# First ticks of layer 0: another order of transposes, folds, gates, logits, flags and loads

## The chip, the cores and the metric

The kernel is one program on one core of a Trainium2 chip. The metric is the device time in microseconds (us) of one execution; lower is better. Five engines run side by side, each with its own list of instructions that it works off in order: TensorE (PE, with its weight loads shown as PEld), VectorE (DVE), ScalarE (ACT), GpSimd (POOL) and SyncE (SP), which here only issues DMAs. Matrix products go from SBUF through PE into PSUM, and ACT or DVE read them from there.

## The reference

The input x (8 sequences of 256 tokens, 128 wide) goes through four layers, and all of them attend to one context ctx of 8 x 64 rows, 64 wide. All data are float32. Layer 0 is what the change touches:

```python
logits = x @ ent_w.T + ent_b                       # one number per token
aw = softmax(logits over the 256 tokens)
read_mask = -sum(aw * log(aw + 1e-9)) > 1.0        # one flag per sequence
q = x @ Wq.T;  k = ctx @ Wk.T + pos;  v = ctx @ Wv.T   # 16 heads of 8
attn = softmax(q k^T * 8**-0.5)                    # over the 64 context rows
memory_output = (attn v) @ Wo.T
pooled = mean of ctx over its 64 rows
h1 = silu([x, pooled] @ gate_w1.T + gate_b1)
gate = sigmoid(h1 @ gate_w2.T + gate_b2)           # one number per token
x = where(read_mask, layernorm(x + gate * memory_output), x)
```

Layer 1 is attention with one head over the same context and adds its result to x. Layer 2 is six times masked self-attention with 16 heads of 64, cross-attention to the context, and a feed-forward block. Layer 3 is one small attention and a last layer norm.

## The kernel before

**Tiles.** x lives in SBUF as `t`, 16 tiles of 128 tokens. For layer 0 it is also turned, into `xT` (128 x 2048), four tiles (one chunk, two sequences) at a time. Products of weights are folded once, before they are used per sequence. `fold_l0` (L513) makes `WVO` from Wv and Wo: it spreads Wo over the 16 heads on POOL (L517), transposes Wv (L522), copies the result twice on ACT (L525), multiplies (L532) and copies from PSUM (L539). `fold_l1`, `fold_l1_values` and `values_l1` (L544 to L589) do the like for layer 1.

**Ticks and phases.** The work is not written in the order in which it runs. `at(tick, phase, fn)` puts a small function into a plan, and at the end of the program the plan is sorted by tick, then phase. Every instruction that a function emits on PE, DVE, ACT or POOL is made to follow the previous one of the plan on that engine (L1199 to L1211). So on these four engines the plan is the order, and an instruction that waits holds up everything behind it on its engine. SP is not in this order; DMAs stand there as the scheduler of the framework puts them.

Sequence b of layer 0 starts at tick 2b: its queries (L635) and its keys spread over heads (POOL, L643) two ticks earlier, then per tick one block of 128 queries: scores (PE, L328, phase 1), lower (ACT copies the scores, L357, DVE takes the maximum, L359, POOL subtracts it, L360, phase 2), exps (ACT, L366, phase 8), a tick later divide (DVE sum L370 and reciprocal L371, POOL product L372), then turn (DVE, L380), then sums (PE, L388). `make_values` (L303, L309) needs `WVO`; `add` (L655) needs `gate`, `normal` and `mix` (L666, L685) need `nflag` and `flag`. Layer 1 of sequence b follows from tick 2b + 7, and the first self-attention projects its keys in tick 13.

The start of the program is `plan_start` (L614). In tick -4 `turn_x` (L431) turns all of x and makes the keys of layer 0 (`k0T`, L407 and L411). In tick 0, after the first scores, come `logits` (L440: DVE builds a selector, PE L447, then DVE and ACT make the softmax, L453 to L459) and `gate_inputs` (L474: mean of the context, L476 and L477, a small product L479, then the hidden values of the gate on PE, L486). In tick 1 come `entropy` (L462, with a logarithm on ACT, L465), `gate_hidden` (L492: for each of eight sequences a sigmoid on ACT, L497, and a multiply on DVE, L498), `fold_l0`, and `gates` (L500: flags, L503, gates, L505, and a sigmoid, L509), then the conversion of the self-attention mask (DVE, L602) and its store to DRAM (SP, L609).

**Buffers.** All PSUM tiles are two banks wide and come from one pool of four, so each new tile waits until the readers of the fourth before it are done. The tags `k`, `q`, `v`, `e` and `o` of SBUF also have four tiles each; the four incoming pieces of the mask take two of `k` and two of `q`. Small operands of the start are cut from two tiles with `place` (L92).

**Loads.** SP issues x, then the constants one after the other, the mask (L190), and the weights of layer 2; ACT's queue issues the context, and the key, position and query weights of layer 0.

Of the kernel before, what the change touches and what calls it, by code (L numbers as in the profile page):

```python
# [16 lines left out]
P = 128  # L17
# [10 lines left out]
def tile_xattn_stack(ctx: ExitStack, tc: tile.TileContext, io, out: bass.AP):  # L28
# [16 lines left out]
    def two_banks(base):  # L45
        return psum.tile([P, 1024], F32, tag="ps", name=uniq(base))
# [4 lines left out]
    def tp_tile():  # L51
        return one_bank("tp")

    def mm_tile():
        return one_bank("mm")

    def big(tag, bufs=4, shape=(P, 1024), dtype=F32):

        return heap.tile(list(shape), dtype, tag=tag, name=uniq(tag), bufs=bufs)
# [4 lines left out]
    def sm(shape, tag):  # L64
        return small.tile(shape, F32, tag=tag, name=uniq(tag))

    def load_const(name, shape):
        t_ = const.tile(shape, F32, tag=name, name=name)
        nc.sync.dma_start(out=t_, in_=io[name])
        return t_  # L70
# [7 lines left out]
    def column(name):  # L78
        v = io[name]
        t_ = const.tile([v.shape[0], 1], F32, tag=name, name=name)  # L80
        nc.sync.dma_start(out=t_, in_=v.unsqueeze(1))
        return t_
# [9 lines left out]
    def place(where, n, rows=P):  # L92
        whole, used = room[where]
        room[where][1] = used + n
        assert used + n <= whole.shape[-1]
        return whole[:rows, used : used + n]

    def load_into(where, name, rows, n, queue=None):
        t_ = place(where, n, rows)
        (queue or nc.sync).dma_start(out=t_, in_=io[name])  # L100
        return t_
# [20 lines left out]
    w0k = load_into("second", "L0_WkT", DM, D, nc.scalar)  # L122
    posT = load_into("second", "L0_posT", D, M, nc.scalar)
    w0q = load_into("second", "L0_WqT", D, D, nc.scalar)
    entw = load_const("L0_entT", [D, 1])
    entb = bcast_rows("L0_ent_b", B)
    w1b = load_into("second", "L0_w1bT", DM, 64)
# [2 lines left out]
    w2g = load_const("L0_w2T", [64, 1])  # L130
    b2g = bcast_rows("L0_gate_b2")
    w0v = load_into("second", "L0_WvT", DM, D)
    w0o = load_into("second", "L0_WoT", D, D)
    nc.sync.dma_start(out=ctx2[DM:], in_=ctx_v)
    ln0_g = column("L0_ln_scale")
    ln0_b = column("L0_ln_bias")

# [43 lines left out]
    for r in range(2):  # L181
        rows = slice(64 * r, 64 * r + 64)
        nc.vector.tensor_copy(hmask8[rows], hmask[rows, 8 * r : 8 * r + 8])


    mask_v = io["mask_BxSxS_ik0"].rearrange("b (h p) k -> p b h k", p=P)
    mask_in = []
    for i, tag in enumerate("kkqq"):
        mask_in.append(big(tag, shape=(P, 2, QT, S), dtype=I32))
        nc.sync.dma_start(out=mask_in[i], in_=mask_v[:, 2 * i : 2 * i + 2])  # L190


    W = {}
# [88 lines left out]
    def copy_to(out_, in_, on_vector=False):  # L282
        if on_vector:
            nc.vector.tensor_copy(out_, in_)
        else:
            nc.scalar.copy(out_, in_)  # L286
# [133 lines left out]
    def small_keys(where, w, bias=None):  # L420
        out_ = place(where, B * M).rearrange("p (b m) -> p b m", b=B)
        keys(w, out_, bias)
        return out_
# [4 lines left out]
    nflag = const.tile([P, B], F32, tag="nflag", name="nflag")  # L428
    cg = const.tile([64, B], F32, tag="cg", name="cg")

    def turn_x():  # L431
        for c in range(NT // 4):
            ps = tp_tile()
            for j in range(4):
                nc.tensor.transpose(ps[:, j * P : (j + 1) * P], t[:, 4 * c + j, :], ident)
            copy_to(xT[:, c * 512 : (c + 1) * 512], ps, c % 2 == 0)
            if c == 1:
                S0["k0T"] = small_keys("second", w0k)

    def logits():  # L440
        esel = place("second", B * B).rearrange("p (a b) -> p a b", a=B)
# [20 lines left out]
    def entropy():  # L462
# [8 lines left out]
        S0["rdiag"] = sm([B, B], "rdiag")  # L471
        nc.vector.tensor_scalar(S0["rdiag"], ident[:B, :B], read, None, ALU.mult)

    def gate_inputs():  # L474
        pooled = sm([DM, B], "pooled")
        nc.vector.tensor_reduce(pooled, ctx_all, AX.X, ALU.add)  # L476
        nc.vector.tensor_scalar(pooled, pooled, 1.0 / M, None, ALU.mult)  # L477
        cg_ps = mm_tile()
        nc.tensor.matmul(cg_ps[:64, :B], lhsT=w1b, rhs=pooled, start=True, stop=True)  # L479
        nc.vector.tensor_scalar(cg, cg_ps[:64, :B], b1g, None, ALU.add)  # L480
        S0["h"] = []
        for half in range(2):
            ps = two_banks("mm")
            for i in range(2):
                c = 2 * half + i
                nc.tensor.matmul(  # L486
                    ps[:64, i * 512 : (i + 1) * 512], lhsT=w1a,
                    rhs=xT[:, c * 512 : (c + 1) * 512], start=True, stop=True,
                )
            S0["h"].append(ps)  # L490
# [8 lines left out]

    def gates():  # L500

        ps = two_banks("mm")
        nc.tensor.matmul(ps[:, 512 : 512 + B], lhsT=ones, rhs=S0["rdiag"], start=True, stop=True)  # L503
        for n in range(NT):
            nc.tensor.matmul(  # L505
                ps[:, n : n + 1], lhsT=S0["hs"][n // 8][:64, (n % 8) * P : (n % 8 + 1) * P],
                rhs=w2g, start=True, stop=True,
            )
        nc.scalar.activation(gate, ps[:, :NT], AF.Sigmoid, bias=b2g)  # L509
        nc.vector.tensor_copy(flag, ps[:, 512 : 512 + B])  # L510
        nc.vector.tensor_scalar(nflag, flag, -1.0, 1.0, ALU.mult, ALU.add)

    def fold_l0():  # L513


        wobd = place("first", H * D).rearrange("p (h d) -> p h d", h=H)
        nc.gpsimd.tensor_tensor(  # L517
            wobd, w0o.unsqueeze(1).to_broadcast([P, H, D]),
            hmask.unsqueeze(2).to_broadcast([P, H, D]), ALU.mult,
        )  # L520
        tps = tp_tile()
        nc.tensor.transpose(tps[:, :DM], w0v, ident[:DM, :DM])  # L522
        wv2 = place("second", P)
        for r in range(2):
            nc.scalar.copy(wv2[:, r * DM : (r + 1) * DM], tps[:, :DM])  # L525
        S0["WVO"] = sb([P, HC, D], "WVO", 1, heap)
        wvo = S0["WVO"].rearrange("p (g a) d -> p a g d", g=2)
        for half in range(2):
            ps = two_banks("mm")
            for i in range(2):  # L530
                a = 2 * half + i
                nc.tensor.matmul(  # L532
                    ps[:, i * 512 : (i + 1) * 512], lhsT=wv2,
                    rhs=wobd[:, 4 * a : 4 * a + 4].rearrange("p h d -> p (h d)"),
                    start=True, stop=True,
                )
            for r in range(2):
                rows = slice(r * DM, (r + 1) * DM)
                nc.scalar.copy(  # L539
                    wvo[rows, 2 * half : 2 * half + 2],  # L540
                    ps[rows].rearrange("p (a g r d) -> p a g r d", a=2, g=2, r=2)[:, :, :, r, :],
                )

    def fold_l1():  # L544

        scale = float(D) ** -0.5
        k1T = S0["k1T"] = small_keys("third", w1k, b1k)
        tps = tp_tile()
        nc.tensor.transpose(tps[:, :P], w1q, ident)
        wqT = place("second", P)  # L550
        nc.scalar.mul(wqT, tps[:, :P], scale)
        ps = mm_tile()
        nc.tensor.matmul(
            ps, lhsT=wqT, rhs=k1T.rearrange("p b m -> p (b m)"), start=True, stop=True
        )
        S0["K1q"] = place("third", B * M).rearrange("p (b m) -> p b m", b=B)
        nc.scalar.copy(S0["K1q"].rearrange("p b m -> p (b m)"), ps)
        S0["bqb"] = place("fourth", P)
        nc.vector.tensor_scalar(S0["bqb"], b1q.to_broadcast([P, P]), scale, None, ALU.mult)

    def fold_l1_values():
        tps = tp_tile()
        nc.tensor.transpose(tps[:, :DM], w1v, ident[:DM, :DM])
        wvT = place("second", DM)
        nc.scalar.copy(wvT, tps[:, :DM])
        bvb = place("second", P)
        nc.vector.tensor_copy(bvb, b1v.to_broadcast([P, P]))
        ps = two_banks("mm")
        nc.tensor.matmul(ps[:DM, :D], lhsT=wvT, rhs=w1o, start=True, stop=True)
        nc.tensor.matmul(ps[:, 512 : 512 + D], lhsT=bvb, rhs=w1o, start=True, stop=True)  # L570
        wvo = place("second", D)
        bvo = place("second", D)
        nc.scalar.copy(wvo[:DM], ps[:DM, :D])
        nc.scalar.copy(bvo, ps[:, 512 : 512 + D])
        S0["wvo1"], S0["bvo"] = wvo, bvo
# [36 lines left out]
            )  # L612

    def plan_start():  # L614
        at(-4, 0, turn_x)
        at(0, 3.0, logits)
        at(0, 3.2, gate_inputs)
        at(1, 3.0, entropy)
        at(1, 3.1, gate_hidden)
        at(1, 3.2, fold_l0)  # L620
        at(1, 3.4, gates)
        for i in range(4):
            at(1, 8.5, lambda i=i: mask(i))
        at(1, 8.6, store_masks)
        at(3, 4, fold_l1)
        at(4, 4, fold_l1_values)
        at(5, 4, values_l1)
        at(16, 6, mask_keys)

    def plan_l0(b, T):  # L630
# [638 lines left out]
```

## Time and profile before

| what | value |
|---|---|
| median of 3 runs | 2530.57 us (2528.28 to 2533.17) |
| the profiled execution | 2528.09 us, of which the span 2526.4 us |
| busy: PE, PEld, DVE, ACT, POOL | 2393.0, 1765.0, 1822.0, 1735.1, 1443.0 us |
| mean granted PE clock | 0.975 |
| chain that ended last, by engine | PE 69%, POOL 13%, DVE 8%, ACT 7%, issue 3% |
| from 0 to 89.9 us | PE busy 60.51, granted clock 0.83 |
| from 89.9 to 300 us | PE busy 199.39, granted clock 0.98 |
| from 300 us to the end (2226.4 us) | PE busy 2133.09, granted clock 0.98 |

The page of the profile divides the span into 40 slices of 63 us and gives each engine's busy share in tenths. The chain that ended last is followed back from the last instruction, at each step to what released it. A row of a wait names the waiting group and its line, the group that released it, the time in all, how often, and the longest. A row of the timeline gives start and duration in us, engine, line, operation, what is written and read, how often, and in brackets the idle time ahead of it and what ended that. PE counts each float32 matmul of the program as two instructions.

### The profile page before, as it was taken

The page shows a single profiled execution, that of the slowest core. Times are in us where ns is not written, and L with a number is a line of the kernel's source. Part 1 is how long each engine was busy: PE and PEld are TensorE (multiplying, and loading weights), DVE is VectorE, ACT ScalarE, POOL GpSimd, SP SyncE. Part 2 cuts the span into 40 slices and gives each one's busy share as a digit, 9 for nine tenths or more (in the row PEclk, how much of TensorE's full clock was granted, in tenths as well). Part 3 has the DMA queues.
Part 4 walks back from the last instruction along what each step waited for, and adds up shares of the span by engine and source line. Part 5 has one row for each costly group of instructions (what it writes and reads, how often), then busy time and mean ns, then how long its engine had stood idle before and what let it go on. Part 6 is the DMA issues. An engine that isn't in the chain of part 4 may idle for free.

```text
span 2526.4 us, 100196 instructions
## 1 busy us (share of the span) xinstructions
PE 2393.0 (95%) x42507; PEld 1765.0 (70%) x42507; DVE 1822.0 (72%) x5976; ACT 1735.1 (69%) x4537; POOL 1443.0 (57%) x2477
## 2 busy tenths in 40 slices
PE   6899999999999999999989999989999989999996
PEld 3566777776777776777776777776777776777774
DVE  3677887748887747887747887747887756888764
ACT  3467777657777657777657777657778657778651
POOL 2655556845556844555854555854555763555763
PEclk8999999999999999999999999999999999999996
DMA  5000012000002000002000102000012000000000
GB/s 161 11 2 20 19 35 64 2 8 24 20 28 65 8 7 24 20 20 70 12 2 21 28 20 70 12 2 20 20 28 70 12 2 20 20 20 12 3 1 17
DMA packets 94770, 64.31 MB, mean 25 GB/s; under 512 B 7729, under 2 KB 90353, under 8 KB 94322
## 3 DMA queue, kind: packets, MB, share of 16 engines
q1 hardware_dynamic: 93874, 57.64, 8.3%
q8 instruction: 334, 5.47, 0.9%
q14 instruction: 114, 0.93, 0.1%
q10 hardware_dynamic: 448, 0.26, 0.0%
HBM read 55.78 MB, written 2.10 MB: 23 GB/s over the span
## 4 chain that ended last, share of the span: by engine, by line
PE 69%; POOL 13%; DVE 8%; ACT 7%; issue 3%; DMA 0%; POOLq 0%; DVEq 0%; SPq 0%; ACTq 0%
PE mm L921 14%; PE mm L829 13%; PE sc L866 12%; PE mm L939 7%; PE mm L848 7%; POOL e L360 6%; PE mm L1071 3%; DVE m L359 3%; PE mm L1088 3%; POOL e L372 3%; ACT e L357 2%; PE mm L388 2%; ACT e L885 2%; PE sc L341 1%; POOL rstd L784 1%
## 5 line engine op out<-in xcount | busy, mean ns | idle before, releaser
L895 POOL TENSOR_SCALAR e<-e,rs 128x256 f32<-128x256 f32 x1536 | 702.5, 478 | 690.8 <-DVE rs L893 682.2
L885 ACT ACTIVATE e<-e,mn 128x256 f32<-128x256 f32 x1536 | 758.3, 495 | 131.0 <-DVE mn L880 130.2
L880 DVE CUSTOM_DVE_ANT_0 e<-sc,nm 128x256 f32<-128x256 f32 x1536 | 542.8, 419 | 122.5 <-PE sc L866 122.3
L905 DVE STREAM_TRANSPOSE eTc<-e 128x512 f32<-128x512 f32 x768 | 519.9, 697 | 66.2 <-POOL e L895 64.6
L921 PE MATMUL mm<-eTc,v 32*64 32x256 f32 x12288 | 381.2, 386 | 18.5 <-ACT AT L1007 8.1
L866 PE MATMUL sc<-k,q 64*32 64x256 f32 x12288 | 378.9, 380 | 5.9 <-DVE mn L880 4.2
L921 PEld LDWEIGHTS mm<-eTc,v 32*64 32x64 f32 x12288 | 284.1, 134 | 112.5 <-issue 27.7
L866 PEld LDWEIGHTS sc<-k,q 64*32 64x32 f32 x12288 | 220.2, 106 | 125.3 <-issue 45.8
L360 POOL TENSOR_TENSOR e<-e,m 128x1024 f32<-128x1024 f32 x112 | 213.1, 1903 | 148.6 <-DVE m L359 141.9
L885 ACT ACTIVATION_READ_ACCUMULATOR e<-e,mn 128x1 f32 x1536 | 286.7, 187 | 0.0
L359 DVE TENSOR_REDUCE m<-sc 128x16 f32<-128x1024 f32 x112 | 137.2, 1225 | 179.4 <-ACT e L357 179.4
L388 PE MATMUL mm<-v,k 128*128 128x128 f32 x1792 | 235.5, 287 | 5.9 <-DVE k L380 5.4
L388 PEld LDWEIGHTS mm<-v,k 128*128 128x128 f32 x1792 | 219.1, 200 | 27.4 <-issue 12.1
L341 PE MATMUL sc<-q,tT 128*32 128x256 f32 x3072 | 217.1, 382 | 0.0
L372 POOL TENSOR_TENSOR e<-e,r 128x1024 f32<-128x1024 f32 x112 | 213.2, 1904 | 0.7 <-DVE r L371 0.7
L366 ACT ACTIVATE e<-e 128x1024 f32<-128x1024 f32 x112 | 119.0, 1062 | 115.8 <-POOL e L360 115.8
L829 PE MATMUL mm<-tT,w_sk 128*128 128x256 f32 x768 | 189.6, 390 | 0.0
L286 ACT COPY v<-mm 128x1024 f32<-128x1024 f32 x96 | 97.2, 1012 | 133.1 <-PE mm L848 133.1
L939 PEld LDWEIGHTS mm<-w_sow,o 128*128 128x128 f32 x1536 | 175.1, 192 | 17.7 <-issue 14.4
L848 PE MATMUL mm<-w_sv,tT 128*32 128x256 f32 x3072 | 185.7, 382 | 0.0
L939 PE MATMUL mm<-w_sow,o 128*128 128x128 f32 x1536 | 183.6, 278 | 1.5 <-ACT WVO L1007 1.5
L829 PE MATMUL mm<-tT,w_sq 128*128 128x256 f32 x768 | 173.6, 379 | 0.0
(210 smaller groups left out, 3521.9 us busy)
## 6 DMA issues: line engine op xcount, KB each, us to landing
nm<-mask_d SPq DMA_DIRECT2D x192, 128.0 KB, 3.0
w_sk<-in_L_sa_kv_dram SPq DMA_DIRECT2D x6, 512.0 KB, 9.4
w_sv<-in_L_sa_kv_dram SPq DMA_DIRECT2D x24, 128.0 KB, 2.4
w_sq<-in_L_sa_q_dram SPq DMA_DIRECT2D x6, 512.0 KB, 3.5
w_sow<-in_L_sa_ow_dram SPq DMA_DIRECT2D x6, 512.0 KB, 4.0
w_ckv<-in_L_ca_kv_dram SPq DMA_DIRECT2D x12, 256.0 KB, 4.2
w_cq<-in_L_ca_q_dram SPq DMA_DIRECT2D x6, 512.0 KB, 4.6
w_cow<-in_L_ca_ow_dram SPq DMA_DIRECT2D x6, 512.0 KB, 4.0
```

The lines of the kernel that those rows point to most:

```text
L360: nc.gpsimd.tensor_tensor(e, e, m.unsqueeze(2).to_broadcast([P, 16, M]), ALU.subtract)
L372: nc.gpsimd.tensor_tensor(tl["e"], tl["e"], r.unsqueeze(2).to_broadcast([P, 16, M]), ALU.mult)
L388: nc.tensor.matmul(ps[:, :D], lhsT=eT[:, s].rearrange("p q x -> p (q x)"), rhs=vw[:, r, k, g, :], start=(s == 0), stop=(s == 7),)
L829: nc.tensor.matmul(ps[:, i * S : (i + 1) * S], lhsT=w[:, c * P : (c + 1) * P], rhs=st["tT"], start=True, stop=True,)
L848: nc.tensor.matmul(ps[32 * a : 32 * a + 32, i, :], lhsT=st["tT"][:, kb * 32 : (kb + 1) * 32], rhs=sv[:, a].rearrange("p g x -> p (g x)"), ...
L866: nc.tensor.matmul(sc[32 * a : 32 * a + 32, r, j, :], lhsT=st["q"][g][rows, a, qb * 32 : (qb + 1) * 32], rhs=st["k"][g][rows, a, :], start ...
L880: nc.vector.tensor_tensor_reduce(e[:, i, :], sc4[:, i, :], st["nm"][:, 2 * jj + i % 2, :], -1.0, 3.0 * BIG, ALU.add, ALU.min, mn[:, i : i ...
L885: nc.scalar.activation(e[:, i, :], e[:, i, :], AF.Exp, scale=-1.0, bias=mn[:, i : i + 1], accum_out=rs[:, i : i + 1],)
L895: nc.gpsimd.tensor_scalar(e[:, i, :], e[:, i, :], rs[:, i : i + 1], 1.0, ALU.mult, ALU.mult)
L905: nc.vector.transpose(eT[:, r, :, 2 * jj : 2 * jj + 2, :], e[:, 2 * r : 2 * r + 2, :].rearrange("p j (k x) -> p k j x", x=32),)
L921: nc.tensor.matmul(ops[a // 2][r * HD : (r + 1) * HD, a % 2, :S], lhsT=st["v"][kb // 4][rows, kb % 4, (2 * g + r) * HD : (2 * g + r + 1) * ...
L939: nc.tensor.matmul(st["ps"][:, j * D : (j + 1) * D], lhsT=st["oT"][c // 4][:, c % 4, j * P : (j + 1) * P], rhs=sow[:, c, :], start=(c == 0 ...
```

## The change

Nothing is computed differently; instructions move to other places of the plan, and some loads to another place or queue.

- `turn_x` turns one chunk. Chunk 0 stays in tick -4, chunks 1 to 3 go to tick 0, around the queries of sequence 1. The keys of layer 0 follow chunk 0.
- `gate_inputs` is cut in three: the mean of the context (`pool_context`, tick -4), its small product (`gate_context`, end of tick 0), and the hidden values (tick 1).
- `fold_l0` is cut in three: the spreading of Wo on POOL (`spread_outputs`, tick -1), the transpose of Wv and the two copies (`turn_values`, tick 1, after `gate_hidden`), and products and copies (`fold_l0`, tick 2).
- `gates` and `flags` become two functions with a PSUM tile each. `gates` goes from tick 1 to 2, `logits` from 0 to 2, `entropy` from 1 to 3, `flags` to 4.
- `fold_l1` and `fold_l1_values` are each cut in two (ticks 3 and 4, 5 and 6), and `values_l1` goes from tick 5 to 7.
- Wo of layer 0 is loaded through ACT's queue instead of SP's; the four mask loads are issued before the layer norm's constants of layer 0, not after the constants of layer 3.

```diff
     w0q = load_into("second", "L0_WqT", D, D, nc.scalar)
+    w0o = load_into("second", "L0_WoT", D, D, nc.scalar)
...
-    w0o = load_into("second", "L0_WoT", D, D)
     nc.sync.dma_start(out=ctx2[DM:], in_=ctx_v)
+
+    mask_v = io["mask_BxSxS_ik0"].rearrange("b (h p) k -> p b h k", p=P)
+    mask_in = []
+    for i, tag in enumerate("kkqq"):
+        mask_in.append(big(tag, shape=(P, 2, QT, S), dtype=I32))
+        nc.sync.dma_start(out=mask_in[i], in_=mask_v[:, 2 * i : 2 * i + 2])
+
     ln0_g = column("L0_ln_scale")
...
-    def turn_x():
-        for c in range(NT // 4):
-            ps = tp_tile()
-            for j in range(4):
-                nc.tensor.transpose(ps[:, j * P : (j + 1) * P], t[:, 4 * c + j, :], ident)
-            copy_to(xT[:, c * 512 : (c + 1) * 512], ps, c % 2 == 0)
-            if c == 1:
-                S0["k0T"] = small_keys("second", w0k)
+    def turn_x(c):
+        ps = tp_tile()
+        for j in range(4):
+            nc.tensor.transpose(ps[:, j * P : (j + 1) * P], t[:, 4 * c + j, :], ident)
+        copy_to(xT[:, c * 512 : (c + 1) * 512], ps, c % 2 == 0)
+
+    def keys_l0():
+        S0["k0T"] = small_keys("second", w0k)
...
+    def pool_context():
+        S0["pooled"] = sm([DM, B], "pooled")
+        nc.vector.tensor_reduce(S0["pooled"], ctx_all, AX.X, ALU.add)
+        nc.vector.tensor_scalar(S0["pooled"], S0["pooled"], 1.0 / M, None, ALU.mult)
+
+    def gate_context():
+        cg_ps = mm_tile()
+        nc.tensor.matmul(cg_ps[:64, :B], lhsT=w1b, rhs=S0["pooled"], start=True, stop=True)
+        nc.vector.tensor_scalar(cg, cg_ps[:64, :B], b1g, None, ALU.add)
...
-        ps = two_banks("mm")
-        nc.tensor.matmul(ps[:, 512 : 512 + B], lhsT=ones, rhs=S0["rdiag"], start=True, stop=True)
+        ps = mm_tile()
...
         nc.scalar.activation(gate, ps[:, :NT], AF.Sigmoid, bias=b2g)
-        nc.vector.tensor_copy(flag, ps[:, 512 : 512 + B])
+
+    def flags():
+
+        ps = mm_tile()
+        nc.tensor.matmul(ps[:, :B], lhsT=ones, rhs=S0["rdiag"], start=True, stop=True)
+        nc.vector.tensor_copy(flag, ps[:, :B])
         nc.vector.tensor_scalar(nflag, flag, -1.0, 1.0, ALU.mult, ALU.add)
...
     def plan_start():
-        at(-4, 0, turn_x)
-        at(0, 3.0, logits)
-        at(0, 3.2, gate_inputs)
-        at(1, 3.0, entropy)
+        at(-4, 0, lambda: turn_x(0))
+        at(-4, 1, keys_l0)
+        at(-4, 2, pool_context)
+        at(-1, 0, spread_outputs)
+        for c in range(1, 4):
+            at(0, 3.1 + 0.1 * c, lambda c=c: turn_x(c))
+        at(0, 3.6, gate_context)
+        at(1, 3.0, gate_inputs)
         at(1, 3.1, gate_hidden)
-        at(1, 3.2, fold_l0)
-        at(1, 3.4, gates)
+        at(1, 3.2, turn_values)
         for i in range(4):
             at(1, 8.5, lambda i=i: mask(i))
         at(1, 8.6, store_masks)
-        at(3, 4, fold_l1)
-        at(4, 4, fold_l1_values)
-        at(5, 4, values_l1)
+        at(2, 3.1, fold_l0)
+        at(2, 3.4, gates)
+        at(2, 3.6, logits)
+        at(3, 4, entropy)
+        at(3, 4.1, fold_l1)
+        at(4, 4, flags)
+        at(4, 4.1, fold_l1_keys)
+        at(5, 4, fold_l1_values)
+        at(6, 4, fold_l1_outputs)
+        at(7, 4, values_l1)
         at(16, 6, mask_keys)
```

The functions cut in two hand their tiles on through `S0`; `fold_l1_keys` begins with the product of the turned and scaled query weights with layer 1's keys (L553) and includes its bias (L559), `fold_l1_outputs` with the products of L569 and L570.

More of the change, by code (lines that the diff above doesn't have):

```diff
@@ L183, in tile_xattn_stack @@
         nc.vector.tensor_copy(hmask8[rows], hmask[rows, 8 * r : 8 * r + 8])
[L186 to L190, printed above, removed]
     W = {}
@@ L472, in entropy @@
         nc.vector.tensor_scalar(S0["rdiag"], ident[:B, :B], read, None, ALU.mult)
-    def gate_inputs():
[L475 to L480, printed above, removed]
+    def pool_context():
[6 more added lines that the diff above has]
+        nc.vector.tensor_scalar(cg, cg_ps[:64, :B], b1g, None, ALU.add)
+    def gate_inputs():
         S0["h"] = []
@@ L509, in gates, with spread_outputs, turn_values, fold_l0 @@
         nc.scalar.activation(gate, ps[:, :NT], AF.Sigmoid, bias=b2g)
-        nc.vector.tensor_copy(flag, ps[:, 512 : 512 + B])
+    def flags():
+        ps = mm_tile()
+        nc.tensor.matmul(ps[:, :B], lhsT=ones, rhs=S0["rdiag"], start=True, stop=True)
+        nc.vector.tensor_copy(flag, ps[:, :B])
         nc.vector.tensor_scalar(nflag, flag, -1.0, 1.0, ALU.mult, ALU.add)
-    def fold_l0():
-        wobd = place("first", H * D).rearrange("p (h d) -> p h d", h=H)
+    def spread_outputs():
+        S0["wobd"] = place("first", H * D).rearrange("p (h d) -> p h d", h=H)
         nc.gpsimd.tensor_tensor(
-            wobd, w0o.unsqueeze(1).to_broadcast([P, H, D]),
+            S0["wobd"], w0o.unsqueeze(1).to_broadcast([P, H, D]),
             hmask.unsqueeze(2).to_broadcast([P, H, D]), ALU.mult,
         )
+    def turn_values():
         tps = tp_tile()
         nc.tensor.transpose(tps[:, :DM], w0v, ident[:DM, :DM])
-        wv2 = place("second", P)
+        wv2 = S0["wv2"] = place("second", P)
         for r in range(2):
             nc.scalar.copy(wv2[:, r * DM : (r + 1) * DM], tps[:, :DM])
+    def fold_l0():
+        wobd, wv2 = S0["wobd"], S0["wv2"]
         S0["WVO"] = sb([P, HC, D], "WVO", 1, heap)
@@ L551, in fold_l1, with fold_l1_keys @@
         nc.scalar.mul(wqT, tps[:, :P], scale)
+        S0["wqT"] = wqT
+    def fold_l1_keys():
+        scale = float(D) ** -0.5
+        k1T, wqT = S0["k1T"], S0["wqT"]
         ps = mm_tile()
@@ L567, in fold_l1_values, with fold_l1_outputs @@
         nc.vector.tensor_copy(bvb, b1v.to_broadcast([P, P]))
+        S0["wvT"], S0["bvb"] = wvT, bvb
+    def fold_l1_outputs():
+        wvT, bvb = S0["wvT"], S0["bvb"]
         ps = two_banks("mm")
```

## The prediction

> **What bounds the kernel now.** I read the page's slices first: where is TensorE not full?
>
> ```profile
> PE   6899999999999999999989999989999989999996
> ...
> PEclk8999999999999999999999999999999999999996
> ```
>
> Each digit is a tenth of busy time in 63 us. Only the first slices are low, so later time is TensorE work that this change leaves alone. Next, the stretches between the first scores of successive ticks (line 328 starts at 11.8, 29.9, 53.9, 58.9, 69.8, 79.7, 89.9, 96.0 and 101.1 us for ticks 0 to 8):
>
> ```profile
> 11.80:29.90 18.10, 12.32 (x60) 4.55 (x60) 4.23 (x17) 1.61 (x3) 2.90 (x2) 0.91 0.49 134
> 29.90:53.90 24.00, 11.19 (x80) 7.06 (x79) 8.76 (x15) 11.59 (x20) 7.50 (x3) 0.72 0.70 195
> ...
> 101.10:160.00 58.90, 54.31 (x620) 39.36 (x619) 40.47 (x87) 35.42 (x67) 41.84 (x41) 0.97 0.01 2
> 160.00:300.00 140.00, 134.58 (x2619) 97.08 (x2622) 113.96 (x433) 105.40 (x330) 73.55 (x150) 0.98 0.06 16
> ```
>
> The columns are the stretch, its length, busy time of PE, PEld, DVE, ACT, POOL, granted clock, DMA share, GB/s. Ticks 0 and 1 take 42.1 us, in which PE is busy 23.5, at a low clock; from 160 us it is busy 96%. PE's waits between 4 and 54 us name the reasons:
>
> ```profile
> PE mm L532 <- ACT eTc L525: 12.8, 1, 12.8
> ...
> PE mm L479 <- issue: 3.0, 1, 3.0
> PE mm L447 <- DVE eTc L444: 2.7, 1, 2.7
> ```
>
> The timeline shows what stands in the 12.8 us:
>
> ```profile
> 31.77 0.28 PE L522 MATMUL tp<-ident,eTc 64*128 64x64 f32 x1
> ...
> 34.76 1.28 ACT L497 ACT_TABLE_LOAD   x1
> ...
> 44.47 0.30 ACT L525 COPY eTc<-tp 128x64 f32<-128x64 f32 x2
> ...
> 44.86 5.11 PE L532 MATMUL mm<-eTc,eTc 128*128 128x512 f32 x8 [12.81 <-ACT eTc L525]
> ```
>
> The fold's little copies (0.30) queue on ACT behind the eight sigmoids of gate_hidden, which alternate with DVE's eight multiplies, about 1.0 us a pair, until 45 us. Gates and tick 2's scores queue on PE behind the fold.
>
> **What the Trainium skill says.** *PSUM — Partial Sum Buffer*, "Engine vs sequencer instructions": engine queues are FIFO and matmuls start in program order. The trace agrees: line 532 holds up line 328. *TensorE: Matmul & The Clock Gate*, "What's actually happening": half clock after some 3.4 us of idling, full after as long a busy time. Here line 532 runs four matmuls at 0.85 us, then four at 0.43. *ScalarE: Activation LUTs*, "What ACT_TABLE_LOAD costs": 1.28 us, plus a drain of 1.38; the trace has the 1.28 and no such drain (the sigmoid starts at 36.05). *DMA: Bandwidth & Descriptors*, "Issuing engines are not separate DMA queues": another issuing queue saves only issue time. So moving w0o to ACT's queue costs about 0.5 us of ACT issue (0.44 to 0.61 each) before 4 us, where ACT is idle until 6.5.
>
> **The change, tick by tick.** I lay the new order out with the durations of the trace, 0.1 us per hand-over, each PSUM tile waiting for the fourth before it.
>
> *Before tick 0.* PE turns only chunk 0 (4.1 to 5.2), then the keys (2.07 cold). They no longer stand behind chunk 1; they start at about 5.7 when w0k lands (issued 1.38, about 4.2 later), queries from 7.8, ACT's scaling to 9.2. spread_keys (1.04) ends by 9.6. Scores of tick 0 at **9.8** (before 11.8). The context mean (0.67+0.17) goes on DVE at 8.5, under this. spread_outputs (3.60 on POOL) runs from 9.6 to 13.2; queued behind it is the subtract of line 360, which cannot start before DVE's maximum at about 15. Free, unless w0o lands after 11.4; issued at 3.1, it should be there by 8.
>
> *Tick 0.* Scores 2.8, chunk 1, queries(1), chunks 2 and 3 (about 1 each), the small gate matmul: PE until **16.1**. The fourth tile back (the scores) is free at about 15. No logits, no wait for the mean: 6.3 us against 18.1.
>
> *Tick 1.* Scores 1.9, gate_inputs 3.65, one transpose 0.28: PE done at **22.0**, 5.9 against 24.0. ACT and DVE lag: copy of the scores until 19.1, maximum until 20.35, sum and reciprocal until 21.75. There the eight pairs begin (6.9 us from first multiply to last in the trace): the last sigmoid ends at 28.2, the multiplies at 28.7, the copies of turn_values at 28.5, then an exp table load and exps(0,1) to 30.9. The masks follow on DVE (4 x 0.65, to 31.3).
>
> *Tick 2.* Its scores run at 22.0 to 23.9 without the gates. Then the fold still waits for those copies: **28.5**, a stall of 4.6 us in place of 12.8. Fold 5.1 (cold as before) to 33.6; ACT's WVO copies (1.17 a half) to 34.8, values 1.1 to 36.0, queries 0.7, gates 3.7 to 40.4, logits 16 x 0.213 = 3.4 (full clock; 5.14 before) to **43.8**. So tick 2 takes 21.8 against 5.0.
>
> *Tick 3.* Scores, sums (2.05), keys of layer 1, one transpose: 5.3, next scores at **49.1** (58.9 to 69.8 before). ACT runs late: sigmoid and exp loads around gates and logits put exps(1,0) at 45.5; the entropy costs another load.
>
> *Ticks 4 to 8.* DVE and ACT set the pace of tick 4: ACT reaches exps(1,1) at 52, DVE the sum of (1,1) at 56.5 and the add of (0,1) at 58, for whose tile fold_l1_keys waits: 10.5. Then 4.7 (tick 5: the outputs' fold no longer waits for bvb's 1.27 within its tick), 8.5 (tick 6: sums, values, fold, mix) and 8.0 (tick 7, with values_l1, 3.3). Tick 8 starts at **80.8**, against 101.1.
>
> The sum by start of scores: 2.0 before tick 0, +11.8 (tick 0), +18.1 (1), -16.8 (2), +5.6 (3), -0.6, +5.5, -2.4, -2.9 (4 to 7): 20.3 us. From tick 8 on the order is the same. I take off 1.3 for hand-overs and cold matmuls that such a layout misses, and forecast **19 us**.
>
> *Priced at nothing.* Table loads: sigmoid, exp, Ln, perhaps exp again; two or three more than the three after the first of before, 2.6 to 3.9 us of ACT. They are in the layout. The masks issue at about 10 us instead of 22, ahead of ln0, layer 1's and the later constants on SP: 2.1 us of issue and 2 MB, at the 247 to 365 GB/s that the DMA view shows from 24 to 45 us some 6 to 8 us of transfers. Their cover: ln0 is needed in tick 5, w1q and w1k in tick 3 (45 us), and the first load of tick 0's load_sa still issues at 24; x, w0v and the gate weights are issued ahead of them. The masks themselves are wanted by DVE at 28.7; issued at 22 they took 6.6 to 8.1 us to land. If they came later than 28.7, DVE would hold up tick 2's maximum one for one. store_masks may go before or after load_ca on SP, which carries no written order; a layer-2 weight is first used at 141 (line 829). Dropping the two-bank tile of gates (flag into its own tile) changes nothing in size.
>
> The profiled execution took 2528.09, a span of 2526.4 and 1.7 around it; its forecast is 2509.1. The median of the runs shown is 2530.57, 2.5 above, so the time is 2530.57 - 19 = **2511.5**.
>
> **Rivals.** *Half comes back* (gain 5 to 13, say 10: 2520.6): tick 2's fold, gates and logits are now one block of 15 us before tick 3's scores, and ACT with its additional loads lags into ticks 3 to 5. For it: my layout gives back 16.8 in tick 2 already; cold matmuls (3.6 for line 328 at tick 5 of before, against 1.9) could add 5 to 8. Against: PE has fewer gaps to cool in. *PE becomes the bound* (gain 25 to 36, say 28: 2502.6): PE's busy time to 89.9 us is 60.5, much of it at half clock; if waits and cold stretches mostly vanish, tick 8 could start near 70. Against: DVE's and ACT's chain in tick 4. *Hidden anyway* (0: 2530.6): ticks 8 to 16 hold a PE of 92% and could be paced by weights; but the last of these was issued at 40.4 and landed within 10 us, and the first use of any is at 141. *Slower* (+8: 2538.6): POOL stands still in spread_outputs until w0o lands. Everything of tick 0 after the maximum waits behind it (line 360, then exps and divide). Each us past 11.4 costs one; it eats the 20 only if w0o lands after some 31 us, and +8 needs 39. x, issued before it, is in by 8.4, so nothing supports this. That the change does not do what it says: DVE, ACT, POOL and PE follow the written order, so no.
>
> **How the numbers follow.** Forecast (gain 13 to 25) 0.68; half 0.14; PE-bound 0.11; no change 0.04; slower 0.03. The unknown costs reach -5 (table loads, cold clock) and +6 (warm fold 3.6 in place of 5.1, DVE less late) about the forecast. Range: gain 9 to 29, which adds about half of each neighbouring case, 0.80: 2501.5 to 2521.5. Faster by over 0.2% (5 us, about what this kernel's measurement tells from nothing; its three runs spread 4.9) 0.93, within 0.04, slower 0.03.
>
> **What would show it.** Right: first scores near 10, 16, 22, 44, 49 us and tick 8 near 81; the wait of the first fold matmul on its copy 4 to 5 us; five or six table loads after the first; the stretch after tick 8 as long as before (101.1 to 160). Wrong: a wait of line 360 on w0o or of a mask operation on its DMA; scores of tick 3 past 55; or a gain at tick 8 that is gone at 160, which would say that something other than PE and the tick chain paces layer 0.

## The result, and the profile after

| | before | after | ratio (95% interval) |
|---|---|---|---|
| median | 2529.43 us (2522.92 to 2533.80, 6 runs) | 2511.18 us (2505.36 to 2514.25, 6 runs) | 0.9926 (0.9908 to 0.9944) |
| profiled execution, span | 2528.09, 2526.4 us | 2511.47, 2509.8 us | |

The medians are 18.2 us apart; 19 was forecast. Single runs of one kernel spread by 9 to 11 us, so a few microseconds can't be read from a single time. What follows is therefore read from the trace, where the start of a tick's first scores (line 328) is a sharp mark:

| first scores of tick | 0 | 1 | 2 | 3 | 4 | 5 | 6 | 7 | 8 |
|---|---|---|---|---|---|---|---|---|---|
| before | 11.8 | 29.9 | 53.9 | 58.9 | 69.8 | 79.7 | 89.9 | 96.0 | 101.1 |
| forecast | 9.8 | 16.1 | 22.0 | 43.8 | 49.1 | 59.6 | 64.3 | 72.8 | 80.8 |
| after | 9.5 | 15.7 | 21.3 | 47.0 | 52.7 | 60.0 | 66.7 | 73.2 | 81.3 |

Lines of this section are those of the changed kernel. Its slices, the two rows that stood low at the start before:

```profile
PE   8999999999999999999999999989999989999996
...
PEclk9999999999999999999999999999999999999996
```

The first slice holds 8 tenths where it held 6, and the second 9 where it held 8; the rest looks as it did. By stretches, from tick to tick and then over ticks 8 to 14 (columns: stretch, length, busy time of PE, PEld, DVE, ACT and POOL, granted clock, DMA share, GB/s):

```profile
9.50:15.70 6.20, 6.19 (x52) 3.67 (x52) 1.44 (x2) 2.01 (x4) 3.66 (x2) 1.00 0.77 241
15.70:21.30 5.60, 5.60 (x42) 2.04 (x41) 2.32 (x4) 4.16 (x5) 3.28 (x3) 1.00 0.66 176
21.30:47.00 25.70, 20.21 (x123) 10.05 (x122) 11.16 (x28) 13.07 (x21) 8.01 (x5) 0.80 0.82 230
47.00:52.70 5.70, 5.25 (x52) 3.24 (x52) 3.52 (x6) 4.58 (x8) 0.78 (x1) 1.00 0.96 170
81.30:135.90 54.60, 50.64 (x571) 37.02 (x571) 36.92 (x77) 31.75 (x57) 37.46 (x36) 0.97 0.01 2
```

Ticks 0 and 1 leave PE no gap. The 1.00 of the first row is not to be trusted: the record of the clock begins at 14 us in this trace, and the scores of tick 0 took 3.64 us, against 1.93 at full clock. Tick 2 has become the long one: 5.5 us idle, and a clock of 0.80. PE's waits up to 54 us, where three waits of 18.5 us stood before:

```profile
PE mm L545 <- ACT eTc L533: 5.4, 1, 5.4
PE tp L434 <- DMA t<-in_x_dram: 4.0, 1, 4.0
PE sc L328 <- POOL q L675: 0.8, 1, 0.8
PE mm L407 <- DMA eTc<-in_L_WkT_dram: 0.5, 1, 0.5
```

The waits for DVE's selector and for the mean are gone; the fold (now line 545) waits 5.4 us instead of 12.8. The timeline of PE in tick 2 (start, duration, engine and line):

```profile
21.31 1.93 PE L328 MATMUL sc<-q,xn 64*32 64x256 f32 x32
28.64 6.65 PE L545 MATMUL mm<-eTc,eTc 128*128 128x512 f32 x8 [5.39 <-ACT eTc L533]
35.22 2.40 PE L303 MATMUL mm<-WVO,ctx 64*32 64x256 f32 x32
...
38.18 4.04 PE L508 MATMUL mm<-L_w2T,k 64*128 64x1 f32 x32
42.15 4.94 PE L447 MATMUL mm<-eTc,eTc 128*8 128x256 f32 x16
```

Tick 2 in finer stretches shows where the clock was low:

```profile
28.60:32.00 3.40, 3.36 (x4) 1.51 (x5) 2.81 (x6) 3.24 (x3) 0.00 (x0) 0.50 0.89 230
32.00:35.30 3.30, 3.30 (x9) 1.09 (x11) 3.27 (x5) 1.16 (x2) 2.11 (x2) 0.60 1.08 349
35.30:37.50 2.20, 2.10 (x32) 0.63 (x32) 1.04 (x10) 1.16 (x2) 2.20 (x2) 1.00 1.16 329
...
38.20:42.10 3.90, 3.90 (x33) 3.90 (x32) 0.00 (x0) 2.06 (x3) 0.00 (x0) 0.92 1.06 291
42.10:45.00 2.90, 2.90 (x9) 0.97 (x10) 0.00 (x0) 1.56 (x2) 0.00 (x0) 0.53 1.09 325
```

After that pause seven of the fold's eight matmuls run slowly (6.65 us in all; 5.11 before), and later part of the logits. The values take 2.40 us, where the next ones take 1.09, but not for the clock, which is full again: about 1.1 us of it is waiting for the second half of WVO, which ACT copies from 35.33 to 36.51.

The gain at tick 8 is 19.7 us; at the first scores of ticks 13 and 15 (135.9 and 156.4 us before) it is 20.4 and 20.5. In the two profiled executions it is still 20.2, 20.1, 19.8 and 19.9 us at the load of the second to fifth layer-2 block's keys, 16.7 at the sixth's and 16.6 at the end. The 3 us go between 1527 and 1909 us, far from any edit; the part on the prediction comes back to them.

### The profile page after: what moved, and what is told of

Its sections match the earlier page's. It is cut to its first block, busy times and chain, and to the rows that moved or that the text cites. A ratio compares the mean times of both kernels' runs of the same rounds, so it can differ in the third digit from the quotient of the medians.

```text
span 2509.8 us, 100205 instructions
## 1 busy us (share of the span) xinstructions
PE 2393.4 (95%) x42507; PEld 1766.2 (70%) x42507; DVE 1821.0 (73%) x5976; ACT 1738.0 (69%) x4540; POOL 1442.8 (57%) x2477
## 4 chain that ended last, share of the span: by engine, by line
PE 69%; POOL 13%; DVE 7%; ACT 7%; issue 3%; POOLq 0%; DVEq 0%; ACTq 0%
PE mm L953 14%; PE mm L861 13%; PE sc L898 12%; PE mm L971 7%; PE mm L880 7%; POOL e L360 6%; PE mm L1103 3%; PE mm L1120 3%; DVE m L359 3%; POOL e L372 3%; PE mm L388 2%; ACT e L357 2%; ACT e L917 2%; PE sc L341 1%; POOL rstd L816 1%
```

## The experiments

My theory: the start is a chain through ACT and DVE as much as through PE. What the change takes from ticks 0 and 1 it keeps only where ACT's or DVE's order lets it, and the slow clock after a pause is part of the price. The rivals: the loads do it; PE's waits alone do it; one of the moves (fold or logits) does it all.

Each run below was timed and profiled once; where a ratio is given, it was timed several times. The mark is the first scores of tick 8: 101.1 us before, 81.3 after. Single profiles differ at this mark too. Two of the runs below (layer 1's folds back, logits ahead of gates) have the changed kernel's order up to the fold, which took 6.65 us there and 6.08 and 5.40 in them; the first of the two has it up to tick 3's scores, and these came 1.4 us later. So a difference of about 1.5 us at a mark shows nothing by itself.

**Loads alone.** The kernel before, with Wo's load on ACT's queue and the masks' loads moved forward, as in the diff above.

> The kernel before with only the loads of the change: Wo of layer 0 through ACT's queue, the four mask loads ahead of the layer norm's constants. My sum prices both at nothing: the scores of tick 8 begin at 101.1 us as before, within 0.7, and the profiled span stays within 4 us of 2526.4. The rival, that the masks or Wo were late before: tick 8 comes 2 us or more earlier.

Measured: tick 8 at 102.1 us, span 2527.5. Tick 1 came 2.2 us earlier (27.7), but tick 2 at 54.2, 0.3 later than before. Tick 8 is 0.3 us beyond what I allowed, by the clock: the fold took 6.71 us here and 5.11 before, behind the same wait of 12.8. So the new loads by themselves bring nothing that this run shows, and cost at most 1 us.

**The start alone.**

```diff
-        at(-4, 0, turn_x)
-        at(0, 3.0, logits)
-        at(0, 3.2, gate_inputs)
+        at(-4, 0, lambda: turn_x(0))
+        at(-4, 1, keys_l0)
+        at(-4, 2, pool_context)
+        for c in range(1, 4):
+            at(0, 3.1 + 0.1 * c, lambda c=c: turn_x(c))
+        at(0, 3.5, logits)
+        at(0, 3.6, gate_inputs)
```

> The kernel before with only a quarter of x turned at first, the other chunks in tick 0, and the mean of the context at tick -4; logits and gate inputs stay in tick 0. By the layout tick 0 begins near 9.5 us, tick 1 near 24 (29.9 before), and the 5.9 us stay to the end of the start: tick 8 near 95 (94 to 96.5). The rival, that a start which is 6 us earlier only waits longer in tick 1 for ACT: tick 8 later than 98.

Measured: ticks 0 to 3 at 9.8, 24.1, 48.1, 53.2 us, tick 8 at 93.7, span 2521.1. The 5.8 us of tick 1 stay, and 1.6 more come in tick 5, where scores and sums ran faster (3.06 and 2.05 us, against 3.64 and 3.00): 7.4 in all, 0.3 beyond the early end of what I gave. A start that is earlier for PE, ACT and DVE alike is kept.

**Fold and gates alone.** The kernel before, with

```diff
-        at(1, 3.2, fold_l0)
-        at(1, 3.4, gates)
+        at(-1, 0, spread_outputs)
+        at(1, 3.2, turn_values)
+        at(2, 3.1, fold_l0)
+        at(2, 3.4, gates)
+        at(2, 3.5, flags)
```

> The kernel before with only layer 0's fold cut in three and fold, flags and gates in tick 2. The sigmoids still start near 36 us, so the fold's products still start near 44.8, but tick 2's scores fill part of the wait: tick 3 near 57.5 (58.9 before), tick 8 at 96 to 99. The rival, that this move is what the change lives on: tick 8 near 90 or earlier.

Measured: tick 2 at 34.6 us (53.9 before), tick 3 at 57.5 (58.9), tick 8 at 96.2, span 2526.8. Of the 19.3 us by which tick 2 comes earlier, 1.5 are left at tick 3 and 4.9 at tick 8. The span shows none of them: from tick 8 to the end this execution took 2430.6 us, against 2425.3 before, in the same order. The fold's move alone is not what the change lives on.

**Layer 1's folds back.** The changed kernel, with

```diff
-        at(4, 4.1, fold_l1_keys)
-        at(5, 4, fold_l1_values)
-        at(6, 4, fold_l1_outputs)
-        at(7, 4, values_l1)
+        at(3, 4.2, fold_l1_keys)
+        at(4, 4.1, fold_l1_values)
+        at(4, 4.2, fold_l1_outputs)
+        at(5, 4, values_l1)
```

> The changed kernel with layer 1's folds back at ticks 3, 4 and 5. My layout has them wait for DVE within a tick there (3.4 us for the keys, 1.4 for the bias in the trace of before): tick 8 at 83.5 to 87 us, against 81.3. The rival, that spreading them over ticks 3 to 7 is only moved work: tick 8 at 81.3 within 0.7.

Measured: tick 3 at 48.4, tick 8 at 91.8 us, span 2522.5: 10.5 us lost. Of these, 1.4 were lost before tick 3, ahead of any instruction that this edit moves. From tick 3 to tick 8 it took 43.4 us, against 34.3: 9.1 us lost, well over what I expected (2.2 to 5.7) and nearly half of the gain. DVE's timeline of this run in tick 3, and then PE's:

```profile
55.90 1.46 DVE L466 TENSOR_TENSOR e<-e 8x256 f32<-8x256 f32 x1
57.40 0.41 DVE L468 TENSOR_REDUCE lmax<-e 8x1 f32<-8x256 f32 x1
...
58.15 0.73 DVE L416 TENSOR_SCALAR o<-mm,L_bk 128x512 f32<-128x512 f32 x1
```

```profile
53.33 0.33 PE L562 MATMUL tp<-ident,eTc 128*128 128x128 f32 x1
59.03 2.04 PE L571 MATMUL mm<-o,eTc 128*128 128x512 f32 x2 [5.38 <-DVE o L577]
61.00 3.63 PE L328 MATMUL sc<-q,xn 64*32 64x256 f32 x32
```

The keys of layer 1 leave PSUM on DVE (L416) only after the entropy's four operations, and PE, whose next instruction is their product (L571), stands for 5.4 us with tick 4's scores behind it (the row names L577, the small DVE instruction right behind L416, as the releaser). Then the scores take 3.63 us, and tick 5's 3.44, instead of 1.93. Over ticks 3 to 7 this run's granted clock is 0.88; the changed kernel's is 1.00. The two pauses (5.4, and 1.3 before L592 a tick later) and the slow matmuls behind them (0.9 for L571, 1.7 and 1.5 for the scores) add up to 10.8 us. The changed kernel has small waits of its own in these ticks. From tick 3 to tick 8 PE is idle for 7.9 us here and 3.1 there, and busy for 35.5 and 31.2 with the same instructions: of the 9.1 us, 4.8 are pauses and 4.3 slow clock. In the changed kernel the product comes a tick later and waits for nothing.

**Logits back.** The changed kernel, with

```diff
-        at(2, 3.6, logits)
-        at(3, 4, entropy)
+        at(0, 3.5, logits)
+        at(1, 2.95, entropy)
```

> The changed kernel with the logits back in tick 0 (behind the turned chunks) and the entropy back in tick 1. PE's 3.5 to 5 us of logits go from tick 2 to tick 0, and the logarithm's table load and 0.5 us go ahead of the sigmoids on ACT: tick 1's scores near 20, the fold near 34.5 (28.6), tick 3 near 48.5 (47.0), then some lighter ticks: tick 8 between 80.5 and 84 us, against 81.3, so that moving the logits is worth little by itself. The rival, that taking the logits out of tick 0 is one of the large parts: tick 8 at 86 or later.

Measured: ticks 1 and 3 at 20.5 and 49.2, tick 8 at 83.3 us, span 2507.2. The fold started at 35.65, 1.15 us later than I wrote; 0.9 of it is DVE, whose entropy operations now stand ahead of the first multiply (ACT's second sigmoid waits 2.12 us for it, 1.22 in the changed kernel). Moving logits and entropy is worth 1.9 us at most, small as expected and little more than single profiles differ by.

**All of x turned first.** The changed kernel with the turns back in tick -4 (chunks 0, 1, keys, 2, 3).

> The changed kernel with all of x turned in tick -4, the keys after the second chunk as before. The first scores begin near 11.8 us in place of 9.5; tick 0 has three chunks less to turn. If ACT's chain (scores, subtract, exps, lower, sigmoids) sets the fold, all of the 2.3 us stay: fold near 30.9, tick 8 near 83.6 (83 to 84.2). The rival, that PE's own work sets the pace: about 1 us, tick 8 near 82.3.

Measured: first scores at 11.8, fold at 30.1, tick 3 at 49.2, tick 8 at 84.8 us, span 2512.6. Neither expectation fits. The fold came 1.45 us later, between the two: the first scores ran partly at full clock here (2.79 us against 3.64), which gave 0.85 of the 2.3 back. At tick 3 the loss is 2.1, at tick 8 3.5, of which 1.3 are slow scores in tick 6 (3.27); without these tick 8 would lie where ACT's chain puts it (83.5). So a quarter of x first is worth 1.5 to 3.5 us; the run doesn't settle which engine sets it.

**Is it PE's wait or ACT's order? Wv turned early.** The changed kernel, with

```diff
-        at(1, 3.2, turn_values)
+        at(1, 2.9, turn_values)
```

> The changed kernel with the transpose of Wv and its two copies ahead of the gate's inputs and sigmoids in tick 1, so that the fold needn't wait for them. The 5.4 us of PE's wait before the fold go. If ACT sets the end of tick 2, WVO's copies still start only at about 32 us, behind exps and lower, and values_of can run from 34.3 in place of 36.6: tick 8 near 79 us (78 to 80), against 81.3. The rival, that the wait of PE itself is what costs: 5 us less, tick 8 near 76.

Measured: tick 3 at 45.8, tick 8 at 80.1 us, span 2505.6. PE's timeline of this run:

```profile
23.17 1.98 PE L545 MATMUL mm<-eTc,eTc 128*128 128x512 f32 x4
25.72 1.95 PE L545 MATMUL mm<-eTc,eTc 128*128 128x512 f32 x4 [0.56 <-DVE k L502]
32.29 3.74 PE L303 MATMUL mm<-WVO,ctx 64*32 64x256 f32 x32 [4.62 <-ACT WVO L552]
```

The wait of 5.4 us before the fold is gone, the fold runs at full clock (3.9 us for both halves, 6.65 in the changed kernel), and 1.2 us are won: a wait of 4.6 us for ACT's copies of WVO has taken its place, and the slow clock goes to the values (3.74). That is less even than the 2.3 of my theory, and no more than single profiles differ by; the rival's 5 us are out.

**Where ACT's time is: two tiles.** The changed kernel, with

```diff
-        for b in range(B):
+        for b in (0, 4, 1, 5, 2, 6, 3, 7):
             h = S0["hs"][b // 4][:64, (b % 4) * S : (b % 4 + 1) * S]
```

> The changed kernel with the eight sigmoids and multiplies of gate_hidden taken in the order 0, 4, 1, 5, 2, 6, 3, 7, so that neighbours read different PSUM tiles. In the trace only the pair 3 to 4, which changes the tile, did not wait. If the shared tile is what makes ACT and DVE alternate, the eight pairs take about 4.2 us in place of 7.6, the fold starts near 25.2 (28.6) and tick 8 comes near 78 us (77 to 79). The rival, that the alternation has another reason: fold at 28.6 and tick 8 at 81.3 within 0.7.

Measured: tick 3 at 40.3, tick 8 at 74.6 us, span 2503.3: 6.7 won, twice what I expected. ACT's sigmoids in the changed kernel's timeline, and then in this run's:

```profile
24.48 0.83 ACT L501 ACTIVATE k<-mm,cg 64x256 f32<-64x256 f32 x2 [0.54 <-DVE k L502]
25.89 0.47 ACT L501 ACTIVATE k<-mm,cg 64x256 f32<-64x256 f32 x1 [0.58 <-DVE k L502]
26.90 0.47 ACT L501 ACTIVATE k<-mm,cg 64x256 f32<-64x256 f32 x1 [0.54 <-DVE k L502]
```

```profile
22.78 0.86 ACT L501 ACTIVATE k<-mm,cg 64x256 f32<-64x256 f32 x2 [0.76 <-DVE k L502]
23.79 0.86 ACT L501 ACTIVATE k<-mm,cg 64x256 f32<-64x256 f32 x2 [0.15 <-DVE k L502]
24.80 0.86 ACT L501 ACTIVATE k<-mm,cg 64x256 f32<-64x256 f32 x2 [0.15 <-DVE k L502]
```

Each sigmoid waited until DVE had done with the previous sequence's part of the same tile; on two tiles they run in pairs, and the waits fall from 4.0 to 1.1 us in all. The Trainium skill bears on this: *PSUM — Partial Sum Buffer*, "PSUM bank collisions raise a hardware error", has software keep two engines off one bank. If that is the reason here, the wait covers the whole tile of two banks: the order from sequence 1 to 2 changes the bank and waited too. The edit alone leaves a rival: the results of the sigmoids lie in two SBUF tiles (`k`), and the new order alternates between these as well. Two places of the changed kernel's trace speak for PSUM. DVE's maximum only reads the scores in PSUM, and still it starts when ACT has ended its copy of them:

```profile
13.22 1.01 ACT L357 COPY e<-sc 128x1024 f32<-128x1024 f32 x1 [4.04 <-PE sc L328]
14.26 1.22 DVE L359 TENSOR_REDUCE m<-sc 128x16 f32<-128x1024 f32 x1 [4.78 <-ACT e L357]
...
15.40 0.68 DVE L284 COPY eTc<-tp 128x512 f32<-128x512 f32 x1
15.57 0.58 ACT L286 COPY eTc<-tp 128x512 f32<-128x512 f32 x1 [0.47 <-PE tp L434]
```

The last two rows write two parts of one SBUF tile (`xT`) from two PSUM tiles, and run at the same time. Still, no run separates the two kinds of tile for the sigmoids themselves. PE's timeline of this run shows the other half of the gain:

```profile
25.93 3.69 PE L545 MATMUL mm<-eTc,eTc 128*128 128x512 f32 x8 [2.35 <-ACT eTc L533]
29.66 2.87 PE L303 MATMUL mm<-WVO,ctx 64*32 64x256 f32 x32
...
36.75 3.62 PE L447 MATMUL mm<-eTc,eTc 128*8 128x256 f32 x16
```

The fold starts 2.7 us earlier. The clock doesn't fall behind the shorter pause (2.35 us, not 5.4), so the fold takes 3.0 less. The logits take 1.3 less, which the order doesn't assure: with Wv turned early besides, they took 5.31 behind the same gates (below).

**Logits ahead of gates.**

```diff
-        at(2, 3.6, logits)
+        at(2, 3.35, logits)
```

> The changed kernel with the logits ahead of the gates in tick 2. The gates' 32 matmuls of one column leave TensorE at half clock: 7 of the logits' 16 matmuls behind them took 0.43 us each, 4.9 us in all. Ahead of the gates they should take about 3.5, but then tick 3's scores stand behind the gates and run at half clock (3.6 in place of 1.9): tick 8 at 81.3 us within 0.7, the slow clock only moves. The rival, that the clock depends on the fold's wait alone: tick 8 at 79.8 or earlier.

Measured: tick 3 at 45.7 us, tick 8 at 82.9, span 2504.8. PE's timeline of this run:

```profile
37.26 3.62 PE L447 MATMUL mm<-eTc,eTc 128*8 128x256 f32 x16
40.81 4.98 PE L508 MATMUL mm<-L_w2T,k 64*128 64x1 f32 x32
45.72 3.64 PE L328 MATMUL sc<-q,xn 64*32 64x256 f32 x32
```

The logits take 1.3 us less, the gates 0.9 and the scores behind them 1.7 more: the slow clock moves, as expected. Tick 8 is 1.6 later and not equal, so I missed there, by more slow matmuls after it (tick 6: 3.42).

**Both edits, and ACT's order.** First the two edits together (Wv early, two tiles).

> The two edits without the third: the fold no longer waits on PE, but WVO's copies still stand behind exps and lower on ACT. If ACT's order is what counts, nothing over the two tiles alone: tick 8 at 74.6 us, between 73.8 and 75.6. The rival, that the 2.35 us which PE still waits with the two tiles are what counts: tick 8 near 72.2.

Measured: tick 3 at 41.4, tick 8 at 75.7 us, span 2501.4. PE's 2.35 us of waiting before the fold are gone, and waits of 0.56 us within the fold and 1.58 for WVO have come. Nothing is won: tick 8 is 0.1 us later even than I gave, with slow logits (5.31, against 3.62 with the two tiles alone). Then with the fold's products and WVO's copies in tick 1, right behind the sigmoids:

```diff
-        at(2, 3.1, fold_l0)
+        at(1, 3.3, fold_l0)
```

> The changed kernel with both of the last edits (Wv turned ahead of the gate's inputs; neighbouring sigmoids on different PSUM tiles) and the fold's products and WVO copies in tick 1, right behind the sigmoids, ahead of exps on ACT. If ACT's order sets tick 2, the WVO copies run from about 25 to 27.4 us (29.0 to 31.4 with the two tiles alone), tick 3's scores come near 37.5 and tick 8 near 72 us, so about 9 us less than the changed kernel's 81.3: near 2502 us, 27 below the kernel before. The rival, that exps pushed behind the copies only move the wait to tick 3: tick 8 at 74.6 or later.

Measured: median 2506.22 us, ratio to before 0.9908 (0.9892 to 0.9925); tick 3 at 41.6, tick 8 at 77.5. ACT's copies did run at 25.4 to 27.8 us as laid out, but tick 3 did not come earlier. PE's timeline of this run:

```profile
29.43 3.73 PE L508 MATMUL mm<-L_w2T,k 64*128 64x1 f32 x32
35.40 6.24 PE L447 MATMUL mm<-eTc,eTc 128*8 128x256 f32 x16 [2.25 <-DVE eTc L444]
41.57 1.93 PE L328 MATMUL sc<-q,xn 64*32 64x256 f32 x32
```

The next engine in line is DVE, whose selector for the logits stands behind a maximum, a sum and two transposes; PE waits 2.25 us for it, and the logits behind run slowly: 6.24 us. The rival of this run was right, if not by its mechanism. So the selector is built by a function of its own, which goes to tick -4, where DVE is idle:

```diff
+        at(-4, 3, select)
```

> The kernel of the three edits with DVE's selector for the logits (a memset and eight small copies, 0.7 us) built in tick -4 in place of tick 2, where PE waited 2.25 us for it and then ran the logits at half clock (6.2 us). If that wait is what took the gain, logits begin near 33.2 us, tick 3's scores near 38 to 38.5 and tick 8 comes near 73 us (72 to 74.5), in place of 77.5. The rival, that the next wait takes its place (DVE's maximum and sum, or ACT's late exps): tick 8 at 76 or later.

Measured: median 2499.77 us (5 runs), ratio to before 0.9878 (0.9860 to 0.9896); tick 3 at 38.6, tick 8 at 74.55 us, 0.05 beyond what I gave. PE's timeline, with the logits on line 450 here:

```profile
29.72 3.73 PE L511 MATMUL mm<-L_w2T,k 64*128 64x1 f32 x32
33.38 5.31 PE L450 MATMUL mm<-eTc,eTc 128*8 128x256 f32 x16
38.62 1.93 PE L328 MATMUL sc<-q,xn 64*32 64x256 f32 x32
```

The wait is gone and tick 3 comes 3 us earlier. This version beats both kernels: its interval lies below that of the change (0.9908 to 0.9944). That all of it is due to the selector isn't shown: the interval of the three edits without it (0.9892 to 0.9925) overlaps this one, and in the trace it is level with the two tiles alone (74.6), of which there is only a single time (2504.99).

## Why the prediction was right, and where its steps were not

- **Ticks 0 and 1** (2.0, 11.8 and 18.1 us booked): right within 0.7 us at each mark. The first scores took 3.64 us, not 2.8, and still the marks came no later than booked.
- **The fold's wait** (4.6 us instead of 12.8): measured 5.4. The reason given, copies behind the sigmoids on ACT, is right. But removing this wait alone brought 1.2 us, since ACT's WVO copies end last there. (ACT was not idle until 6.5 us in the kernel before, as I read: its first table load stood at 3.14. In the changed kernel it stands at 3.62, behind the new load's issue, and ACT's next work is at 8.79.)
- **Tick 2** (21.8 us booked): mis-sized by 3.9; it took 25.7. The terms: the stall 5.4 instead of 4.6, fold 6.65 instead of 5.1, gates 4.0 instead of 3.7, logits 4.9 instead of 3.4. The values' wait for WVO was booked rightly (2.4 us with the copies in front). Most of the rest is slow clock, for which, with hand-overs, I had taken 1.3 us off the whole sum. I took the fold's 5.11 from before, where the clock came back 2.9 us after its start; here it came back after 6.0. And I booked the logits at full clock. How much of this is chance the repeats show: the fold took 5.40 to 6.65 us in three runs of one order.
- **Tick 4** (10.5 us booked): mis-sized the other way; it took 7.3. I had fold_l1_keys wait for the add of block (0,1), by the rule that a PSUM tile waits for the fourth before it. In the changed kernel's trace its product starts at 58.98 us and that add (L687) at 61.10. So the tile reused was one released sooner, and the wait didn't exist. It was most likely the values' tile: ACT's copy of the values (L309) ends at 58.76, and in two of the runs (logits back, logits ahead of gates) the product waits 0.23 us for just this copy. So the rule of the fourth tile, given above under the buffers, doesn't hold throughout. This error and tick 2's cancel, and so do ticks 5 and 6 (4.7 and 8.5 us booked, 6.7 and 6.5 taken; PE waited 1.6 us of tick 5 for ACT's normal, L701). That tick 8 came within 0.5 us is in part luck.
- **Layer 1's folds** (folded into ticks 4 to 7, where the sum nets -0.4 us): taking them back costs 9.1 us. The sum compared with the kernel before, tick by tick, and so hid that without this part the other moves would have lost nearly half of their gain again. It did name the waits that go; it didn't price the clock behind them.
- **Priced at nothing**: the loads, within 1 us (first experiment). Table loads: six after the first, as against five or six. POOL's spreading didn't hold up line 360, which started at 15.57, when DVE's maximum was ready. The masks had landed when DVE wanted them at 28.8.
- **The rivals.** "Half comes back": tick 2 did give back 3.9 us more than booked, tick 4 returned 3.2. "PE the bound": not at 81 us; with the later edits tick 8 came to 74.6, so part of that room exists. "Hidden anyway" and "slower": out, since the gain of 20 us is whole at 156 us.
- **The last 3 us** (20.5 us in the trace at tick 15, 16.6 at the end of the profiled execution): no step of mine has it. It lies between 1527 and 1909 us in one pair of executions, and there the clock tells. Of the slices of 20 us from 1500 to 1900, two stood below full clock before (0.93 and 0.98) and three after (0.91, 0.93 and 0.89): worked out from these, some 4 and 11 us at half clock, which makes about 3.5 us. From tick 8 on the order is the same in all fourteen profiled executions, and this rest took 2421.5 to 2430.7 us, with 88 us at half clock in the shortest and 112 in the longest. So these 3 us are of the size by which executions of one order differ; the six-run medians give 18.2.

## What to carry to other kernels

Where four engines follow one written order, lay the new order out for each of them: taking away PE's longest wait (5.4 us) brought 1.2, while reordering eight sigmoids so that ACT and DVE take turns on two tiles brought 6.7 in one run, 2.7 of it by an earlier fold and the rest by a clock that stayed full. Price a pause of PE by its length and by the matmuls that run slowly behind it; in layer 1's folds the two were about equal. And try each part in the company of the others: the layer 1 part looked like nothing in a tick-by-tick sum and held 9 of 20 us.

## What the runs showed of the hardware that was not expected

- A slow clock comes and goes in steps of 3.4 us. In the changed kernel the granted clock is one half from 27.8 to 34.6 us and from 41.4 to 44.85, in the kernel before from 34.1 to 47.8: 6.8, 3.4 and 13.7 us, or two, one and four such steps. So what a pause costs depends on where the steps fall. Behind a pause of 5.4 us the fold had 6.0 us of half clock, behind 12.8 us in the kernel before only 2.9. The Trainium skill, *TensorE: Matmul & The Clock Gate*, "What's actually happening", has 3.4 us of full work release the clock, in windows that run freely. The traces agree: in the changed kernel the fold began 0.8 us after the start of one step, which didn't release the clock, and the next, full of work, did.
- Matmuls of one column can lower the clock like a pause. Behind the gates (32 of them, about 4 us with PE shown busy throughout) the next matmuls ran at half clock, in whole or in part, in every run but one: in the changed kernel the clock fell at 41.4 us, before the gates had ended (logits 4.94 us), and with the selector early it fell 1 us behind them, though PE had had no idle time since 26 us (logits 5.31). The exception is the run with the two tiles alone (logits 3.62, full clock). That the steps of the clock lay otherwise there is likely, but not shown.
- In this program a PSUM tile that ACT and DVE both only read is read by one after the other: DVE's maximum of the scores starts 0.03 us after ACT's copy ends (14.26 and 14.23 us).
